# Channel mix on Trainium2: the order of work written by hand on four engines, and six PSUM banks for the quarter products

## The chip, the cores and the metric

The kernel runs on one core of a Trainium2 chip. A core has TensorE (matrix products, results in PSUM banks), VectorE and GpSimd (elementwise work), ScalarE (activations and copies), and queues from which SyncE starts DMA transfers. In the profile they are PE (with PEld for its weight loads), DVE, POOL, ACT and SP. The metric is the time of one execution on the device in microseconds (us); the time of a kernel is the median over several executions.

## The reference, cut to what matters

A batch of 8 sequences of 512 tokens with 512 channels goes through two layers, each a cross attention followed by a feed-forward part; each part adds its gated output to x. The change is in the last part, the channel mix (`_L1_ffn_ref`), and in the attention in front of it:

```python
x = x + tanh(g_xattn[1]) * _L1_xattn_ref(layernorm(x), ctx, ctx, mask, ...)
x = x + tanh(g_ffn[1]) * _L1_ffn_ref(layernorm(x), W_r, W_k, W_v, mu_r, mu_k)

# _L1_ffn_ref, for each sequence x of shape (512 tokens, 512 channels):
x_prev = x shifted by one token, with zeros in front
xr = mu_r * x + (1 - mu_r) * x_prev
xk = mu_k * x + (1 - mu_k) * x_prev
r = sigmoid(xr @ W_r.T)
k_act = square(relu(xk @ W_k.T))
out = r * (k_act @ W_v.T)
```

All of it is float32.

## The kernel before

**Stages.** x stays in SBUF for the whole kernel, as 32 tiles of 128 tokens. The program runs the first attention, a routed feed-forward part, the second attention, and the channel mix. Each attention is a loop over the 32 tiles. One pass of it is called a slot here, and it works on several tiles at once: the normalization of one tile, the scores of another, the transposed probabilities (`tps`, L328) and the output (`ops`, L363) of others. On VectorE a slot has the maxima of the scores (L303), the subtraction (L304), the sums (L309), the reciprocals (L316), the addition to x (L372), and the statistics of the layer normalization (`layernorm_stats`: L50 and L51, with small steps on GpSimd at L53 to L55, and two buffers for its temporary `bnst`); ScalarE makes the exponentials (L307) and copies (L333, L346), and GpSimd scales the probabilities (L317).

**The channel mix** handles one sequence ("batch" b, four tiles) at a time in three stages, each one product of two 512 x 512 matrices: the keys (k), the gates (g) and the values (v). k is xk times W_k, followed by Relu (L1010) and Square (L1011) on ScalarE, in the tile `kT`. g is xr times W_r, followed by Sigmoid (L1020) on ScalarE, in `r`. v is kT times W_v, followed on VectorE by the product with r (L1032) and by the gated addition to x (L1034, a scalar_tensor_tensor). Two finished quarters side by side are written to the output by one DMA of 512 KB (L1038).

What a batch needs ahead of that: the normalized tiles `xn` (ScalarE, L952), their transposes (TensorE into the bank `xnps`, L966; ScalarE copies them to `yT`, L967), and the mixes xk and xr in four chunks 0 to 3 each: a chunk is one scaled copy on ScalarE (L981) and one scalar_tensor_tensor on VectorE (L984). The four transposes of the tiles of a batch are called tr0 to tr3 here.

**Seven products.** Each stage multiplies with seven products of 256 x 256 quarters instead of eight. A quarter fits one PSUM bank (128 partitions x 512 elements). The left matrix gives A11, A12, A22 and four sums S1 to S4, the right one B11, B21, B22 and T1 to T4; these sums are made of quarters by additions and subtractions (`left`, L791 to L794; `right`, L802 to L805): by VectorE for kT (S), xr (`xrs`, S) and xk (`xks`, T), and once for the weights, by GpSimd for W_v and W_k and by VectorE for W_r. The products are called p1 to p7, and k.p3 is product p3 of the keys:

- p1 = A11 B11: ScalarE copies its bank (L839)
- p6 = S2 T2: VectorE adds it to p1 (L844), giving u2
- p7 = S3 T3: VectorE adds it to u2 (L849), giving u3
- p2 = A12 B21: VectorE adds it to p1 (L853): quarter 00 is finished
- p5 = S1 T1: ScalarE copies its bank (L860). GpSimd adds it to u2 (L861) and to u3 (L862): quarter 11 is finished
- p4 = A22 T4: VectorE subtracts it (L867): quarter 10 is finished
- p3 = S4 B22: VectorE adds it (L872): quarter 01 is finished

The order is p1, p6, p7, p2, p5, p4, p3. Each product is four matmuls of 128 x 256 at L824 (two halves of rows, two of the summed dimension); the profile shows each float32 matmul as two, so a product stands as x8. The intermediate results lie in temporaries `ctmp`. The banks of the products come from the pool `at_mm` with the tag mm, which has four and which the transposes use too. The pool `at_s`, two tiles of two banks each with the tag s, holds the attention's scores and is not used in the mix after the attention's end.

**The order of the work.** Within the attention and the mix, TensorE executes what it is given in the order of the program text (`tc.manual_schedule(engines={PE})`). The order of VectorE, ScalarE and GpSimd is chosen by the framework's scheduler, which can also move an instruction ahead of others that were written earlier. Once compiled, each engine executes its own queue in order, and an instruction that waits holds up all that stand behind it. The output DMAs and the loads are started from SP's queue.

The channel mix begins inside the last slots of the attention (`in_slot`): weights are loaded, the first eight tiles get their statistics, batch 0 is normalized, transposed and mixed, and the keys of batch 0 begin. After the last slot `run` does batch after batch: in the keys the statistics and the tiles of the next batch, of which three are transposed there and the fourth in the gates; after that the xk chunks and the sums of the next batch, then the xr chunks and sums, and the values.

Of the kernel before, what the change touches and what calls it, by code (L numbers as in the profile page):

```python
# [9 lines left out]
FP = mybir.dt.float32  # L10
# [7 lines left out]
P = 128  # L18
# [758 lines left out]
class SevenProducts:  # L777
# [9 lines left out]
    @staticmethod  # L787
    def left(w, sums, engine):

        s1, s2, s3, s4 = sums  # L790
        engine.tensor_tensor(s1, quarter(w, 0, 1), quarter(w, 1, 1), ALU.add)  # L791
        engine.tensor_tensor(s2, s1, quarter(w, 0, 0), ALU.subtract)
        engine.tensor_tensor(s3, quarter(w, 0, 0), quarter(w, 0, 1), ALU.subtract)
        engine.tensor_tensor(s4, quarter(w, 1, 0), s2, ALU.subtract)  # L794
        own = [quarter(w, 0, 0), quarter(w, 1, 0), quarter(w, 1, 1)]
        return dict(zip(SevenProducts.LEFT, own + [s1, s2, s3, s4]))

    @staticmethod
    def right(w, sums, engine):

        t1, t2, t3, t4 = sums
        engine.tensor_tensor(t3, quarter(w, 1, 1), quarter(w, 0, 1), ALU.subtract)  # L802
        engine.tensor_tensor(t1, quarter(w, 0, 1), quarter(w, 0, 0), ALU.subtract)
        engine.tensor_tensor(t2, quarter(w, 1, 1), t1, ALU.subtract)
        engine.tensor_tensor(t4, t2, quarter(w, 1, 0), ALU.subtract)  # L805
        own = [quarter(w, 0, 0), quarter(w, 1, 0), quarter(w, 1, 1)]
        return dict(zip(SevenProducts.RIGHT, own + [t1, t2, t3, t4]))

    def __init__(self, nc, at, a, b, finish):

        self.nc, self.at, self.a, self.b, self.finish = nc, at, a, b, finish
        self.pieces = iter(
            [self.p1, self.p6, self.p7, self.p2, self.p5, self.p4, self.p3]
        )
# [5 lines left out]
    def multiply(self, a, b):  # L820
        ps = self.at.p_mm.tile([P, 2, 256], FP, name="cps", tag="mm")
# [11 lines left out]
    def temporary(self, n):  # L833
        return self.at.pool.tile([P, 2, 256], FP, name="ctmp", tag=f"v{n}")

    def p1(self):
        ps = self.multiply("A11", "B11")
        self.q1 = self.temporary(0)
        self.nc.scalar.copy(self.q1, ps)  # L839

    def p6(self):
        ps = self.multiply("S2", "T2")
        self.u2 = self.temporary(1)
        self.nc.vector.tensor_tensor(self.u2, self.q1, ps, ALU.add)  # L844

    def p7(self):
        ps = self.multiply("S3", "T3")
        self.u3 = self.temporary(2)
        self.nc.vector.tensor_tensor(self.u3, self.u2, ps, ALU.add)  # L849

    def p2(self):
        ps = self.multiply("A12", "B21")
        self.nc.vector.tensor_tensor(self.q1, self.q1, ps, ALU.add)  # L853
        self.finish(0, 0, self.q1)

    def p5(self):
        nc = self.nc
        ps = self.multiply("S1", "T1")
        q5 = self.temporary(3)
        nc.scalar.copy(q5, ps)  # L860
        nc.gpsimd.tensor_tensor(self.u2, self.u2, q5, ALU.add)  # L861
        nc.gpsimd.tensor_tensor(q5, self.u3, q5, ALU.add)  # L862
        self.finish(1, 1, q5)

    def p4(self):
        ps = self.multiply("A22", "T4")
        self.nc.vector.tensor_tensor(self.u3, self.u3, ps, ALU.subtract)  # L867
        self.finish(1, 0, self.u3)

    def p3(self):  # L870
        ps = self.multiply("S4", "B22")
        self.nc.vector.tensor_tensor(self.u2, self.u2, ps, ALU.add)  # L872
        self.finish(0, 1, self.u2)


class ChannelMix:
# [5 lines left out]

    def __init__(self, cm, tc, es, ins, gate, out):
        self.cm, self.nc, self.tc, self.es = cm, cm.nc, tc, es
        self.ins, self.gate, self.out = ins, gate, out
        self.xn, self.yT, self.mix, self.sums = {}, {}, {}, {}

    def start(self):
# [12 lines left out]
        self.wk7 = SevenProducts.left(self.wk, [sums[:, i] for i in range(4)], nc.gpsimd)  # L901
# [5 lines left out]
    def sum_weights(self):  # L907
# [3 lines left out]
        self.wr7 = SevenProducts.right(self.wr, [sums[:, i] for i in range(4)], nc.vector)  # L911
# [3 lines left out]
        self.wv7 = SevenProducts.right(self.wv, sums, nc.gpsimd)  # L915
        self.kTs = [both[:, i] for i in range(3, 7)]

    def in_slot(self, s, attention, late):

        self.at = attention  # L920
        if not late:
            if NT - 1 <= s:
                self.k7.next(2)
            return
        if s == -1:
            self.start()
        if NT - 14 <= s < NT - 6:
            layernorm_stats(self.cm, self.at.norm, s - (NT - 14))
# [6 lines left out]
        if 0 <= i < TB:  # L935
            self.normalize(i)
        if s in (NT - 3, NT - 2):
            self.mixes(0, 1, slice(2 * (s - NT + 3), 2 * (s - NT + 3) + 2))
        if s == NT - 2:
            self.sum_mix(0, 1)  # L940
# [3 lines left out]
        if s == NT:  # L944
            self.sum_weights()
            self.mixes(0, 0)
            self.sum_mix(0, 0)

    def normalize(self, t):
        nc, cm = self.nc, self.cm  # L950
        self.xn[t] = xn = self.at.norm.tile([P, D], FP, name="xn")
# [17 lines left out]
    def mixes(self, b, m, chunks=slice(0, NC)):  # L969

        nc, yT = self.nc, self.yT[b]
        if chunks.start == 0:
# [7 lines left out]
        for c in range(NC)[chunks]:  # L980
            nc.scalar.activation(  # L981
# [197 lines left out]
```

## Time and profile before

| | |
|---|---|
| median of three runs | 1501.27 us (1497.16 to 1504.57) |
| the profiled execution | 1501.78 us, span in the trace 1499.6 us |
| mean granted TensorE clock | 0.99 |
| TensorE busy | 1420.2 us (95% of the span) |
| VectorE busy | 1034.0 us (69%) |
| ScalarE busy | 721.4 us (48%) |
| GpSimd busy | 547.8 us (37%) |
| in the mix alone (1200 to 1499.6 us): TensorE, VectorE, ScalarE, GpSimd busy | 281.6, 207.5, 133.4, 64.5 us |

Times in the trace count from the start of the span. The second attention ends near 1160 us; its last slots and the keys and gates of batch 0 lie between 1144 and 1200 us. From 1200 us on a batch takes some 40 us.

How the lines are to be read: a row of the page's slices has one digit for each fortieth of the span (37.5 us), the busy share in tenths. A line of the timeline gives the start, the duration, the engine, the line of the program, the operation, the names of what it writes and reads with their shapes, the count of merged instructions, and in brackets the idle time in front of it with what ended it. A line of the chain of waits gives start, duration, engine, and what the chain of work that ended last passes through.

### The profile page before, as it was taken

Reading aid. Unit: us, or ns where it says so; the run is one execution under the profiler, and the core shown is the slowest. Engines: PE = TensorE matmul, PEld = TensorE weight load, DVE = VectorE, ACT = ScalarE, POOL = GpSimd, SP = SyncE. Lnnn points to the kernel's source line nnn. Section 1 sums busy time; section 2 is a strip of 40 time slices with the busy share of each in tenths; the row PEclk is TensorE's granted clock in tenths of the full one; section 3 lists DMA queues with packets and bytes.
Section 4 is the critical chain, followed back from the end, with each engine's and each line's share of the span. In section 5 each row is a group of like instructions: output and inputs, shape, how many; then the busy total and the mean of one; then the engine's idle time right before and its main releaser. Section 6 shows DMA issues by size and latency. Waiting matters only on the chain.

```text
span 1499.6 us, 30719 instructions
## 1 busy us (share of the span) xinstructions
PE 1420.2 (95%) x13344; PEld 1003.2 (67%) x13344; DVE 1034.0 (69%) x1382; ACT 721.4 (48%) x983; POOL 547.8 (37%) x585
## 2 busy tenths in 40 slices
PE   7999999999988998999899999999997999999997
PEld 3456666666666787888545666666564788888886
DVE  3457777777777676766716777777778777777774
ACT  2246565565544445444224555555555455444432
POOL 2514333333333001555844554455335312222212
PEclk9999999999998999999999999999998999999999
DMA  9200000000000437433201000000000000000000
GB/s 303 86 9 22 22 22 23 22 23 23 22 22 23 131 121 235 119 100 96 100 0 56 2 1 1 1 2 1 1 30 1 1 28 29 29 28 28 29 29 29
DMA packets 44329, 69.33 MB, mean 46 GB/s; under 512 B 2859, under 2 KB 19755, under 8 KB 44195
## 3 DMA queue, kind: packets, MB, share of 16 engines
q1 hardware_dynamic: 43907, 67.37, 13.9%
q8 instruction: 105, 1.72, 0.5%
q14 instruction: 29, 0.24, 0.0%
q10 hardware_dynamic: 288, 0.00, 0.0%
HBM read 50.59 MB, written 16.78 MB: 45 GB/s over the span
## 4 chain that ended last, share of the span: by engine, by line
PE 75%; DVE 14%; ACT 5%; POOL 3%; issue 2%; DMA 1%; POOLq 0%; ACTq 0%; DVEq 0%
PE qps L255 15%; PE ops L363 13%; PE cps L824 9%; PE tps L328 7%; PE s L289 4%; PE aps L346 4%; PE vps L197 4%; PE rps L733 3%; PE kps L178 3%; PE ops L754 2%; PE l1ps L648 2%; PE xnps L246 2%; PE rlps L475 2%; DVE xk L984 2%; PE gps L621 2%
## 5 line engine op out<-in xcount | busy, mean ns | idle before, releaser
L317 POOL TENSOR_TENSOR pr<-pr,rs 128x1920 f32<-128x1920 f32 x64 | 217.6, 3400 | 451.6 <-ACT prT L333 348.2
L363 PE MATMUL ops<-wo,aT 128*128 128x512 f32 x512 | 243.1, 598 | 2.3 <-ACT aT L354 2.3
L255 PE MATMUL qps<-xnT,wq 128*128 128x512 f32 x512 | 236.3, 603 | 1.4 <-ACT xnT L247 1.4
L307 ACT ACTIVATE pr<-pr 128x960 f32<-128x960 f32 x128 | 128.3, 1003 | 207.5 <-DVE pr L304 207.3
L303 DVE TENSOR_REDUCE mx<-s 128x8 f32<-128x960 f32 x128 | 142.2, 1152 | 105.5 <-PE s L289 105.5
L309 DVE TENSOR_REDUCE sm<-pr 128x8 f32<-128x960 f32 x128 | 147.6, 1153 | 24.9 <-ACT pr L307 24.5
L255 PEld LDWEIGHTS qps<-xnT,wq 128*128 128x128 f32 x512 | 92.1, 189 | 101.1 <-issue 93.2
L328 PEld LDWEIGHTS tps<-ident,pr 128*120 128x120 f32 x1024 | 120.0, 142 | 58.6 <-issue 44.7
L363 PEld LDWEIGHTS ops<-wo,aT 128*128 128x128 f32 x512 | 92.4, 192 | 92.0 <-issue 88.1
L328 PE MATMUL tps<-ident,pr 128*120 128x128 f32 x1024 | 129.7, 281 | 21.0 <-DVE pr L304 17.9
L304 DVE TENSOR_TENSOR pr<-s,mx 128x960 f32<-128x960 f32 x128 | 141.6, 1148 | 0.0
L333 ACT COPY prT<-tps 120x1024 f32<-120x1024 f32 x128 | 124.1, 1015 | 36.4 <-PE tps L328 36.4
L746 POOL TENSOR_TENSOR r<-r,b 128x1024 f32<-128x1024 f32 x32 | 75.9, 2377 | 148.9 <-ACT r L745 148.9
L372 DVE SCALAR_TENSOR_TENSOR x<-ops,gates,x 128x512 f32<-128x512 f32 x64 | 48.1, 751 | 94.8 <-PE ops L363 94.8
L861 POOL TENSOR_TENSOR ctmp<-ctmp 128x512 f32<-128x512 f32 x24 | 33.6, 1401 | 202.8 <-DVE ctmp L849 96.8
L50 DVE BATCH_NORM_STATS2 bnst<-x 128x6 f32<-128x512 f32 x128 | 85.0, 685 | 17.2 <-DMA x<-in_x_dram 15.2
L247 ACT COPY xnT<-xnps 128x512 f32<-128x512 f32 x64 | 37.7, 589 | 81.7 <-PE xnps L246 81.7
L54 POOL TENSOR_TENSOR rstd<-ve,mhalf 128x1 f32<-128x1 f32 x128 | 72.0, 564 | 6.1
L346 PE MATMUL aps<-prT,v 120*32 120x128 f32 x2048 | 70.0, 276 | 2.4 <-ACT prT L333 2.4
L289 PE MATMUL s<-kT,qT 32*128 32x120 f32 x2048 | 71.1, 275 | 0.0
L289 PEld LDWEIGHTS s<-kT,qT 32*128 32x128 f32 x2048 | 65.6, 186 | 6.4 <-issue 6.3
L733 PE MATMUL rps<-ident,rT 128*128 128x128 f32 x512 | 61.9, 275 | 5.6 <-DVE rT L713 5.6
(141 smaller groups left out, 2490.2 us busy)
## 6 DMA issues: line engine op xcount, KB each, us to landing
w<-in_w_dram SPq DMA_DIRECT2D x32, 512.0 KB, 5.2
x<-in_x_dram SPq DMA_DIRECT2D x8, 1024.0 KB, 15.6
aside<-x SPq DMA_DIRECT2D x32, 256.0 KB, 2.0
x<-aside SPq DMA_DIRECT2D x8, 1024.0 KB, 10.5
out_dram<-x SPq DMA_DIRECT2D x16, 512.0 KB, 2.9
ctx<-in_ctx_dram SPq DMA_DIRECT2D x4, 960.0 KB, 11.7
wk<-in_wk_dram SPq DMA_DIRECT2D x3, 1024.0 KB, 9.3
wv<-in_wv_dram SPq DMA_DIRECT2D x3, 1024.0 KB, 5.4
```

The source lines that it names most:

```text
L255: nc.tensor.matmul(ps, self.wq[:, c, f * P : (f + 1) * P], self.xnT[b][:, c, :S], start=(c == 0), stop=(c == NC - 1),)
L289: nc.tensor.matmul(s[j // 2][:, j % 2, hc * LK : (hc + 1) * LK], self.qT[b][r : r + 32, hc, toks], self.kT[r : r + 32, hc, keys], start=no ...
L303: nc.vector.tensor_reduce(mx, sv, AX.X, ALU.max)
L304: nc.vector.tensor_tensor(pv, sv, mx.to_broadcast([P, 2, NC, LK]), ALU.subtract)
L307: nc.scalar.activation(pv, pv, AF.Exp, scale=SM_SCALE)
L309: nc.vector.tensor_reduce(sm[:, 2 * u : 2 * u + 2, :], pr[:, 2 * u : 2 * u + 2, :, :], AX.X, ALU.add,)
L317: nc.gpsimd.tensor_tensor(pr, pr, rs.to_broadcast([P, 4, NC, LK]), ALU.mult)
L328: nc.tensor.transpose(ps[:, jj, hc * P : (hc + 1) * P], pr[:, 2 * u + jj, hc, :], self.cm.ident,)
L333: nc.scalar.copy(prT[:, 2 * u : 2 * u + 2, :, :], ps.rearrange("p j (h t) -> p j h t", t=P),)
L346: nc.tensor.matmul(aps[32 * j : 32 * j + 32, hc, :], self.v[b // 2][:LK, b % 2, h * HD : (h + 1) * HD], prT[:, j, hc, :], start=True, stop ...
L363: nc.tensor.matmul(ops, self.aT[t][:, c, :], self.wo[:, c, :], start=(c == 0), stop=(c == NC - 1),)
L824: self.nc.tensor.matmul(ps[:, m, :], self.a[a][:, k, m * P : (m + 1) * P], self.b[b][:, k, :], start=(k == 0), stop=(k == 1),)
```

## The change

In the products:

- They write their results in place: the quarters of `kT`, of `r`, and, for the values, of two tiles `cv` take the part of the temporaries. p5's copy has a tile of its own (`q5`).
- The order is p1, p2, p6, p5, p7, p4, p3; in the values of the last batch p1, p6, p5, p7, p4, p3, p2. GpSimd's two additions follow p7 instead of p5.
- `bank()`: when the attention is over, every third product takes a bank of the tag s; the others take mm as before.

In the values: one scalar_tensor_tensor on VectorE makes c x gate x r (L1092), and a second instruction adds it to x (L1095): on GpSimd, and in the last batch's upper two quarters on VectorE. The last batch writes each finished quarter by its own DMA of 256 KB (L1100); the other batches write two quarters at a time as before (L1104).

In the order of the work: the statistics of all tiles move into the slots of the attention, tile s - 2 into slot s. `stage` hands out a list of other work among the seven products of a stage: in the keys of a batch its own xr chunks and their sums; in the gates the four transposes of the next batch, the sums of kT, and the next xk chunks; in the values the sums of these, and the normalizations of the batch after that. `mix.run()` is executed in the order of the text on TensorE, VectorE, ScalarE and GpSimd.

New line numbers: the products are at L848, the copies of p1 and p5 at L858 and L871, VectorE's additions at L862 (p2), L867 (p6), L875 (p7), L882 (p4) and L887 (p3), GpSimd's at L876 and L877; Relu and Square at L1068 and L1069, Sigmoid at L1079; normalization at L994, the copy to yT at L1009, the chunks at L1022 and L1025.

```diff
 class SevenProducts:
-    def left(w, sums, engine):            # four tensor_tensor at once
+    def left_steps(w, s1, s2, s3, s4, engine):   # a list of four steps
+        return [
+            step(s3, a11, a21, ALU.subtract),
+            step(s1, a21, a22, ALU.add),
+            step(s2, s1, a11, ALU.subtract),
+            step(s4, a12, s2, ALU.subtract),
+        ]
...
-    def __init__(self, nc, at, a, b, finish):
-        self.pieces = iter(
-            [self.p1, self.p6, self.p7, self.p2, self.p5, self.p4, self.p3]
-        )
+    def __init__(self, nc, psum, a, b, c, spare, finish=None, order="1265743"):
+        self.q1 = c[0, 1] if order.index("2") < order.index("6") else c[0, 0]
+        self.pieces = iter([getattr(self, "p" + n) for n in order])
...
     def multiply(self, a, b):
-        ps = self.at.p_mm.tile([P, 2, 256], FP, name="cps", tag="mm")
+        ps = self.psum()
...
+    def p5(self):
+        self.q5 = self.spare()
+        self.nc.scalar.copy(self.q5, self.multiply("S1", "T1"))
     def p7(self):
-        ps = self.multiply("S3", "T3")
-        self.u3 = self.temporary(2)
-        self.nc.vector.tensor_tensor(self.u3, self.u2, ps, ALU.add)
+        nc, u2, u3 = self.nc, self.c[0, 1], self.c[1, 0]
+        nc.vector.tensor_tensor(u3, u2, self.multiply("S3", "T3"), ALU.add)
+        nc.gpsimd.tensor_tensor(self.c[1, 1], u3, self.q5, ALU.add)
+        nc.gpsimd.tensor_tensor(u2, u2, self.q5, ALU.add)
     def p4(self):
-        ps = self.multiply("A22", "T4")
-        self.nc.vector.tensor_tensor(self.u3, self.u3, ps, ALU.subtract)
-        self.finish(1, 0, self.u3)
+        ps, c21 = self.multiply("A22", "T4"), self.c[1, 0]
+        self.finish(1, 1, self.c[1, 1])
+        self.nc.vector.tensor_tensor(c21, c21, ps, ALU.subtract)
+        self.finish(1, 0, c21)
...
 class ChannelMix:
     def in_slot(self, s, attention, stage):
-        if NT - 14 <= s < NT - 6:
-            layernorm_stats(self.cm, self.at.norm, s - (NT - 14))
+        if 0 <= s - 2:
+            layernorm_stats(self.cm, self.at.norm, s - 2)
...
         if s == NT:
+            self.k7.next()
+            layernorm_stats(self.cm, self.at.norm, NT - 1)
             self.sum_weights()
...
+            for t in range(TB, 2 * TB):
+                self.normalize(t)
...
+    def bank(self):
+        self.banks += 1
+        if self.alone and self.banks % 3 == 0:
+            ps = self.at.p_s.tile([P, 2, 512], FP, name="cps2", tag="s")[:, 0, :]
+            return ps.rearrange("p (m c) -> p m c", m=2)
+        return self.at.p_mm.tile([P, 2, 256], FP, name="cps", tag="mm")
...
     def values(self, b):
         def finish(i, j, c):
-            rv = quarter(r, i, j)
-            nc.vector.tensor_tensor(rv, c, rv, ALU.mult)
             xs = quarter(x, i, j)
-            nc.vector.scalar_tensor_tensor(xs, rv, self.gate, xs, ALU.mult, ALU.add)
+            nc.vector.scalar_tensor_tensor(
+                c, c, self.gate, quarter(r, i, j), ALU.mult, ALU.mult
+            )
+            (nc.vector if last and i == 0 else nc.gpsimd).tensor_tensor(xs, xs, c, ALU.add)
...
+        order = "1657432" if last else "1265743"
...
+    def stage(self, product, work):
+        for n in range(7):
+            product.next()
+            for _ in range(-(-len(work) // (7 - n))):
+                work.pop(0)()
...
     def run(self):
+        self.alone = True
         for b in range(B):
             if b > 0:
-                for t in ahead:
-                    layernorm_stats(self.cm, self.at.norm, t)
+                self.stage(self.keys(b), chunks(b, 0) + sums(b, 0))
...
+            squares = SevenProducts.left_steps(self.kT, *self.kTs, self.nc.vector)
+            work = list(squares)
+            if more:
+                tiles = [(TB * (b + 1) + i,) for i in range(TB)]
+                work = calls(self.transpose, *tiles) + work + chunks(b + 1, 1)
+            self.stage(self.gates(b), work)
+            work = []
+            if more:
+                work += sums(b + 1, 1)
+            if b + 2 < B:
+                work += calls(self.normalize, *[(TB * (b + 2) + i,) for i in range(TB)])
+            self.stage(self.values(b), work)
...
-    with ExitStack() as es, tc.manual_schedule(engines={mybir.EngineType.PE}):
+    with ExitStack() as es:
...
+        with tc.manual_schedule(engines={mybir.EngineType.PE}):
+            CrossAttention(...).run()
+        engines = mybir.EngineType
+        with tc.manual_schedule(
+            engines={engines.PE, engines.DVE, engines.Activation, engines.Pool}
+        ):
+            mix.run()
```

## The prediction

> **What bounds the kernel now.** I read the page first: the busy rows, the slices, the chain. Then the chain in order of time for the last stage, and the timeline of one batch there, engine by engine.
>
> ```profile
> PE 1420.2 (95%) x13344; PEld 1003.2 (67%) x13344; DVE 1034.0 (69%) x1382; ACT 721.4 (48%) x983; POOL 547.8 (37%) x585
> ...
> PE   7999999999988998999899999999997999999997
> ...
> PEclk9999999999998999999999999999998999999999
> ```
>
> TensorE is busy 95% of the span at full clock. The channel mix has the last 300 us (slices 33 to 40). The chain there:
>
> ```profile
> 1312.93 2.65 DVE xk L984 x4
> ...
> 1352.90 2.65 DVE xk L984 x4
> ```
>
> Every 40 us the chain leaves TensorE for VectorE, which makes the xk chunks there before it empties the bank that TensorE waits for. The timeline of TensorE, one batch earlier, has that wait in brackets:
>
> ```profile
> 1274.67 1.89 PE L824 MATMUL cps<-wrs,xr 128*128 128x256 f32 x8
> 1278.06 1.99 PE L824 MATMUL cps<-wr,xrs 128*128 128x256 f32 x8 [1.49 <-DVE ctmp L849]
> 1279.89 1.89 PE L824 MATMUL cps<-wv,kT 128*128 128x256 f32 x8
> 1281.61 3.62 PE L824 MATMUL cps<-wvs 128*128 128x256 f32 x16
> 1285.07 1.24 PE L824 MATMUL cps<-wv,kT 128*128 128x256 f32 x5
> ```
>
> Two products take 1285.07 - 1281.61 = 3.46, one 1.727 us; four transposes of a tile take 0.435. A batch of 21 products and 4 tiles needs 38.0 us of TensorE. It takes 39.98 (v.p1 at 1279.89 and next at 1319.87). The 2.0 between are one wait per batch: g.p3 needs the bank of g.p7, and VectorE empties it (L849) late. From v.p1 of batch 0 (1200.65) to that of batch 7 (1478.30) it is 277.65 us; TensorE alone would need 147 x 1.727 + 24 x 0.435 = 264.3. So **13.4 us are to be had there**.
>
> The second thing to see is how VectorE and GpSimd get in each other's way:
>
> ```profile
> 1289.85 1.58 POOL L861 TENSOR_TENSOR ctmp<-ctmp 128x512 f32<-128x512 f32 x1 [2.51 <-DVE ctmp L849]
> 1291.52 1.60 POOL L862 TENSOR_TENSOR ctmp<-ctmp 128x512 f32<-128x512 f32 x1
> ```
>
> ```profile
> 1290.23 0.68 DVE L853 TENSOR_TENSOR ctmp<-ctmp,cps 128x512 f32<-128x512 f32 x1
> 1290.94 1.04 DVE L1032 TENSOR_TENSOR r<-ctmp,r 128x512 f32<-128x512 f32 x1
> 1292.02 1.64 DVE L1034 SCALAR_TENSOR_TENSOR x<-r,gates,x 128x512 f32<-128x512 f32 x1
> 1293.59 0.68 DVE L1032 TENSOR_TENSOR r<-ctmp,r 128x512 f32<-128x512 f32 x1
> ```
>
> L853 has one input in PSUM and runs its 0.68 beside L861. L1032 and L1034 have both inputs in SBUF: each ends 0.55 after the GpSimd instruction in front of it (1291.43 + 0.55 = 1291.98; 1293.12 + 0.54 = 1293.66). L862 in turn is stretched from 1.26 to 1.60 by L1032. Such instructions exclude each other whole, and take turns.
>
> **The change part by part.** A queue walk: each engine's compiled order, each instruction at the later of its queue and its producers. Durations from the tile views: VectorE 0.68 (next one 0.60 later), scalar_tensor_tensor 0.745 (0.67), GpSimd 1.26 (1.35), ScalarE 0.57 to 0.62 for copies, Relu, Square, Sigmoid, 0.71 for a mix chunk; a product is read 0.2 after its end. For before, this walk gives 39.94 per batch against 39.98 measured, with the wait at g.p3: the method holds to 0.1 us.
>
> *Steady batch.* TensorE's work is unchanged, 38.0. Six banks instead of four: g.p3 no longer waits for g.p7. VectorE loses little: a finished quarter of the values cost 0.68 + 0.745, and now costs one scalar_tensor_tensor of 0.745; the add of x (4 per batch) goes to GpSimd, 1.26 each, which has 10 such adds instead of 6. What is late next, in us from the start of g.p1:
> - The third transpose, tr2, needs the bank of k.p3, emptied at 5.7: 1.46 late. tr3 needs the bank of g.p1, whose copy stands on ScalarE behind the last Relu and Square of the keys (each waits for its quarter): 1.27 late. So g.p7 ends at 13.3, not 10.6.
> - g.p7 is added by VectorE until 14.2; GpSimd's two adds follow, the first until 16.0 (held by xk chunk 0), and hold xk chunk 1 until 16.6. ScalarE has Sigmoids in front of mix chunks 2 and 3: each waits for VectorE's g.p4 (17.2) and g.p3 (19.9), so the last xk chunk ends at 21.9, 5 us after the gates' products.
> - VectorE then works without a break: T3, T1, v.p2 and its gate step, T2, v.p6, T4, v.p7 until 27.6. Then quarter 11 from GpSimd (29.0), gate step, v.p4, gate step, v.p3, gate step until 33.2, two of them held by the adds of x. The next xr chunks 0 and 1 are held by the last two adds of x: 34.9 and 36.6, where they would be done by 34.5.
> - k.p2 (37.2), Relu, Square and mix chunks 2 and 3 on ScalarE, k.p7 until 42.4, GpSimd until 44.1, k.p4, S2 (held until 46.0), k.p3 until 46.66. That frees tr2 of the next batch: 46.72 - 5.78 = **40.94 us per batch**.
>
> At this spot a rule of the Trainium skill can be weighed. GPSIMD Engine Reference, Key points: VectorE is structurally about 2x faster in elementwise work, and the two contend where VectorE has two SBUF inputs; no price is given for that. It speaks against the moved add. By the 2x alone, the adds would lie beside VectorE's work on an engine that is 37% busy, and the walk without their exclusion gives 38.0: 13.4 us won. By the rows above each add stops a VectorE instruction, and the walk gives 40.94. I take the rows. The page Perfetto Trace Analysis, Identifying Performance Opportunities, takes consistent bubbles as a sign of too little PSUM: by it, too, two more banks would give 38.0. The row says that L849 is late because of VectorE's queue; two banks more move the wait to tr2.
>
> Six periods of 40.94 and the last (no transposes, no chunks ahead) of 38.2 are 283.8, against 277.65: **+6.2 us**.
>
> *Handover, 1144 to 1200.*
>
> ```profile
> 1151.21 1.59 POOL L803 TENSOR_TENSOR wv<-wv 128x512 f32<-128x512 f32 x1
> ```
>
> ```profile
> 1155.03 3.64 PE L328 MATMUL tps<-ident,pr 128*120 128x128 f32 x16 [6.92 <-DVE pr L304]
> ```
>
> The compiled order puts one more VectorE subtraction (the sum T3 of batch 0) ahead of the maximum (L303, at 1151.61 now) that tps follows. GpSimd's L803 holds it until 1153.4: the maximum and tps start 1.7 later, the idle is 8.6. Given back afterwards: 1.0 and 0.7 of TensorE's waits at 1184.9 and 1197.1, and small ones, since the tiles of batch 1 are normalized earlier and the banks are six. v.p1 of batch 0 comes at 1200.1 instead of 1200.65: **-0.5**, between -2 and +2.
>
> *Tail.* The last order ends with p2, and writes quarters. From v.p1: products end at 12.1, VectorE, which has 11 steps after v.p7 and is held by four GpSimd instructions, at 17.2; before 1495.69 - 1478.30 = 17.4. From there to the end of the span it was 3.9 with 512 KB; the page has 2.9 for 512 KB and 2.0 for 256 KB (aside<-x): 3.0 to 3.9, I take 3.5. **-0.6**.
>
> *Attention.* The statistics for the mix now share two buffers with the attention's own from slot 2 on; the order shows 16 of the attention's no longer hoisted ahead of it, and 19 slots with two statistics where before only three slots held two. Such a slot before:
>
> ```profile
> 839.71 1.29 DVE L50 BATCH_NORM_STATS2 bnst<-x 128x6 f32<-128x512 f32 x2
> 840.91 0.30 DVE L51 BATCH_NORM_AGGREGATE mv<-bnst 128x2 f32<-128x6 f32 x2
> 841.57 2.22 DVE L303 TENSOR_REDUCE mx<-s 128x8 f32<-128x960 f32 x2 [0.36 <-PE s L289]
> ```
>
> VectorE still waits 0.36 for TensorE, and the slot is 11.46 as without: **0**. Were that cover gone, 16 slots x at most 0.8 = 13 us. Quarters written in place, Relu and Square in place: the same instructions, 0. The four normalizations in a row (2.9) lie in ScalarE's idle from 24.4 to 30.8. SP's two last transfers become four; before them nothing on its queue is moved past anything, and nobody waits for the others.
>
> Sum: 0 - 0.5 + 6.2 - 0.6 = +5.1. The profiled execution took 1501.78 (span 1499.6 and 2.2 around it), so 1506.9; it stands 0.5 over the median of 1501.27: **1506.5**. A measurement here can tell about 0.5% from no change, 7.5 us: below 1493.8 is faster, above 1508.8 slower.
>
> **The rivals.**
> 1. *TensorE sets the pace* (faster). About 5 us per batch of the loop are holds between VectorE and GpSimd. If 2.9 of them don't come, the loop falls under 38.0 and the banks do their work: 264.3 instead of 277.65, with the rest -14.5, so 1487. For it: VectorE's work is 27 us of 38, GpSimd's 13. Against: L1034 at 1.64, and xr chunks (L984) of up to 3.88 in the tile view.
> 2. *GpSimd gets the better of the turns* (slower). If its next add starts without the gap of 0.09, the walk gives 41.5; if a held VectorE instruction needs 0.1 more to restart, 41.6; both some 42. From 41.3 on it is over the 0.5%. 7 x 0.6 to 1.1 more: 1511 to 1515. Against: the turns alternate in the rows above.
> 3. *The loop closes as before* (no change): ScalarE or GpSimd a little quicker than walked, 40.0 per batch; only handover and tail count: 1500.
>
> **How the numbers follow.** Forecast 0.46 (1502 to 1511; 0.32 of it below 1508.8), GpSimd's turns 0.22, the loop as before 0.16, TensorE's pace 0.16 (with part of the holds left, 1487 to 1496; 0.13 of it below 1493.8). Faster 0.13; same 0.03 + 0.16 + 0.32 = 0.51; slower 0.14 + 0.22 = 0.36. The range leaves out most of rival 1 and the upper end of rival 2: 1493 to 1515.
>
> **What would show it.** Right: TensorE waits of 1 to 1.5 us before the third and fourth transposes of each gates stage, released by k.p3's add (L887) and g.p1's copy (L858); v.p1 to v.p1 40.9; xr chunks 0 and 1 at 1.7 us beside L1095; idle of 8 to 9 us before tps at 1156. Wrong: v.p1 to v.p1 under 39.5, no waits before transposes, L1095 beside unstretched chunks; or slots of the attention above 11.46.

## The result and the profile after

The changed kernel takes 1506.03 us (median of 8 runs, 1504.21 to 1510.9) against 1499.07 us of the kernel before (8 runs, 1497.16 to 1504.57): the ratio is 1.0046, with a 95% interval of 1.0032 to 1.0060. It is slower by 0.46%, clear of the noise by this interval; that lies inside the 0.5% that the prediction called no change, close to its edge. The forecast was 1506.5.

The page after, the same three rows as before:

```profile
PE 1417.3 (94%) x13344; PEld 1001.0 (67%) x13344; DVE 1045.6 (70%) x1352; ACT 724.6 (48%) x983; POOL 591.4 (39%) x615
...
PE   7999999999988998999899999999997999999997
...
PEclk9999999999999999999999999999998999999999
```

VectorE has 30 instructions fewer than before and is busy 11.6 us longer; GpSimd has 30 more and is busy 43.6 us longer. TensorE does the same work. The timeline of TensorE in one gates stage of the changed kernel (start, duration, instruction; in brackets the idle time in front of it and what ended it):

```profile
1310.88 0.66 PE L1008 MATMUL xnps<-ident,xn 128*128 128x128 f32 x4 [1.32 <-DVE kT L887]
1312.68 0.66 PE L1008 MATMUL xnps<-ident,xn 128*128 128x128 f32 x4 [1.14 <-ACT r L858]
1313.17 5.44 PE L848 MATMUL cps<-wrs,xrs 128*128 128x256 f32 x24
1318.45 1.89 PE L848 MATMUL cps<-wrs,xr 128*128 128x256 f32 x8
```

The old wait before g.p3 is gone (`cps<-wr,xrs` follows without brackets). In its place the third and fourth transposes wait for their banks, the one for k.p3's add (L887), the other for g.p1's copy (L858): 2.46 us per batch where 1.49 stood. v.p1 follows v.p1 after 40.98 us (1280.90, 1321.91, 1362.89, ...).

Where the loop is tight is read from the chain of waits between two such transposes (start, duration, what the chain passes through; "issue" is time in which an engine waits for nothing that the profile shows):

```profile
1337.60 0.69 DVE cv L887
1338.28 0.02 issue
1338.31 1.26 DVE cv L1092
1339.57 2.34 DVE xr L1025 x2
1341.91 0.61 DVE kT L862
1342.52 0.02 issue
1342.54 0.64 ACT kT L1068
...
1343.74 0.71 ACT xr L1022
...
1345.15 0.68 DVE kT L867
...
1347.01 0.69 DVE kT L875
...
1347.83 1.60 POOL kT L876
```

In the order of the text VectorE finishes the values of a batch (L1092), makes two xr chunks of the next one (L1025), and only then empties k.p2's bank (L862). ScalarE makes Relu and Square of that quarter (L1068, L1069) before it can turn to xr chunk 2 (L1022), and VectorE, which is given that chunk ahead of k.p6's add (L867), waits for it. The additions that GpSimd makes meanwhile show why L1092 and L1025 are long. Timeline of GpSimd, and below it VectorE's gate step of quarter 11, a little earlier:

```profile
1333.96 1.27 POOL L877 TENSOR_TENSOR cv<-cv,q 128x512 f32<-128x512 f32 x1
...
1337.76 1.27 POOL L1095 TENSOR_TENSOR x<-x,cv 128x512 f32<-128x512 f32 x1 [0.63 <-DVE cv L1092]
1339.65 1.71 POOL L1095 TENSOR_TENSOR x<-x,cv 128x512 f32<-128x512 f32 x1 [0.63 <-DVE cv L1092]
```

```profile
1334.03 1.74 DVE L1092 SCALAR_TENSOR_TENSOR cv<-cv,gates,r 128x512 f32<-128x512 f32 x1 [1.44 <-POOL cv L876]
```

The add at 1337.76 ends at 1339.03; VectorE's L1092 that began at 1338.31 ends 0.54 later. The add at 1339.65 overlaps the two xr chunks, which take 2.34 instead of the 1.4 of two chunks that nothing holds. The gate step of quarter 11 is held by L877, GpSimd's second addition of p5: it takes 1.74 instead of 0.75 and ends 0.54 after it.

### The profile page after: what moved, and what is told of

Same layout as the page of the kernel before. It is cut to its first block, busy times and chain, and to the rows that moved or that the text cites. A ratio compares the mean times of both kernels' runs of the same rounds, so it can differ in the third digit from the quotient of the medians.

```text
span 1504.1 us, 30766 instructions
## 1 busy us (share of the span) xinstructions
PE 1417.3 (94%) x13344; PEld 1001.0 (67%) x13344; DVE 1045.6 (70%) x1352; ACT 724.6 (48%) x983; POOL 591.4 (39%) x615
## 4 chain that ended last, share of the span: by engine, by line
PE 77%; DVE 11%; ACT 5%; issue 4%; POOL 3%; DMA 1%; POOLq 0%; ACTq 0%
PE qps L255 15%; PE ops L363 13%; PE cps L848 10%; PE tps L328 7%; PE aps L346 4%; PE s L289 4%; PE vps L197 4%; PE kps L178 4%; PE rps L733 3%; PE ops L754 2%; PE l1ps L648 2%; PE xnps L246 2%; PE rlps L475 2%; PE gps L621 2%; PE l2ps L700 1%
## 5 line engine op out<-in xcount | busy, mean ns | idle before, releaser
L303 DVE TENSOR_REDUCE mx<-s 128x8 f32<-128x960 f32 x128 | 142.2, 1152 | 96.1 <-PE s L289 96.1
L1095 POOL TENSOR_TENSOR x<-x,cv 128x512 f32<-128x512 f32 x30 | 43.9, 1465 | 62.7 <-DVE cv L1092 62.7
## 6 DMA issues: line engine op xcount, KB each, us to landing
x<-aside SPq DMA_DIRECT2D x8, 1024.0 KB, 10.6
```

Source lines behind the costliest of these rows:

```text
L303: nc.vector.tensor_reduce(mx, sv, AX.X, ALU.max)
```

## The experiments

All were timed against the kernel before on the same chip, whose median in these groups lay between 1498.9 and 1501.7; "ratio" is that to the kernel before, with its 95% interval (medians of different groups compare less well), and "period" is the distance of v.p1 from v.p1 in the middle batches of the profile. "From first to last" is v.p1 of batch 0 to v.p1 of batch 7.

| kernel | median us | ratio | period us | first to last us |
|---|---|---|---|---|
| before | 1499.07 | 1 | 39.98 | 277.65 |
| changed | 1506.03 | 1.0046 (1.0032 to 1.0060) | 40.98 | 284.19 |
| e1, adds of x on VectorE | 1512.08 | 1.0076 (1.0059 to 1.0093) | 41.35 | 290.12 |
| e2, four banks | 1508.32 | 1.0048 (1.0033 to 1.0064) | 41.48 | 287.17 |
| e7, before with six banks | 1494.81 | 0.9964 (0.9952 to 0.9975) | 39.98 | 272.80 |
| e8, no adds of x | 1488.75 | 0.9924 (0.9906 to 0.9942) | 38.46 | 267.03 |
| e3, transposes apart | 1498.24 | 0.9992 (0.9984 to 1.0000) | 39.70 | 276.50 |
| e4, p5's adds on VectorE | 1495.45 | 0.9976 (0.9968 to 0.9985) | 39.69 | 275.11 |
| e5, transposes and chunks | 1490.60 | 0.9939 (0.9925 to 0.9952) | 38.54 | 268.48 |
| e6, e5 with e4 | 1484.43 | 0.9895 (0.9879 to 0.9910) | 38.02 | 264.36 |
| e9, other last order | 1506.87 | 1.0053 (1.0037 to 1.0070) | 40.98 | 285.87 |
| e11, scheduler's order | 1486.18 | 0.9916 (0.9900 to 0.9933) | 38.01 | 264.33 |
| e13, e6 with four banks | 1488.39 | 0.9920 (0.9905 to 0.9935) | 38.65 | 268.19 |
| e15, e6 with e1 | 1486.14 | 0.9900 (0.9878 to 0.9922) | 38.02 | 264.36 |

**Is it the moved add?** e1 gives the adds of x back to VectorE, and e8 leaves them out.

```diff
-            (nc.vector if last and i == 0 else nc.gpsimd).tensor_tensor(xs, xs, c, ALU.add)
+            nc.vector.tensor_tensor(xs, xs, c, ALU.add)
```

> The changed kernel with the additions to x (L1095) on VectorE in every batch; GpSimd keeps only its six additions per batch. Queue walk: VectorE has no break between the gates and the end of the values, so 4 x 0.6 us more on its queue delay the xr chunks, k.p3's add and the bank of the third transpose: 41.6 us per batch (wait before the third transpose 2.1, before the fourth 1.3), tail 0.8 longer; some 5.5 us slower than the changed kernel, 1511.5. Rival (the moved add is what costs, because GpSimd and VectorE exclude each other): with the adds back on VectorE the loop falls to between 38.0 and 39.98 us per batch, 1487 to 1499.

It became slower, not faster: 1512.08 us. The wait before the third transpose grew from 1.3 to 1.66; the fourth kept its 1.14. So the rival falls that moving the adds is what costs: undoing the move makes the loop longer, by 0.37 us per batch. Only 2.4 us of the 5.9 by which its way from first to last is longer are the loop; the other 3.5 are two stretches of slow TensorE in its profile (last section). GpSimd's other six additions still hold VectorE in e1 (quarter 11's gate step takes 1.74 there too); e4 below takes these away. The row of stretches tells why the move gives VectorE so little (busy us and count of TensorE, its weight loads, VectorE, ScalarE, GpSimd, then clock, DMA share and GB/s; first the changed kernel, then e1):

```profile
1281.00:1322.00 41.00, 38.54 (x186) 33.50 (x185) 30.40 (x40) 20.12 (x34) 14.61 (x12) 1.00 0.07 26
```

```profile
1281.00:1322.00 41.00, 38.20 (x184) 33.20 (x183) 30.26 (x43) 20.11 (x34) 8.33 (x8) 1.00 0.07 26
```

In 41 us VectorE is busy 30.4 with the adds moved away and 30.3 with them: what it saves it loses again, held by the very adds that it gave away. (With the adds on VectorE the last two gate steps take 0.75 each and the pair of xr chunks 1.41, against 1.27, 1.26 and, in the same view, 2.41.) That the 0.4 us per batch that the move is still worth come from where the held time falls is not shown.

```diff
-            (nc.vector if last and i == 0 else nc.gpsimd).tensor_tensor(xs, xs, c, ALU.add)
+            if last:
+                nc.vector.tensor_tensor(xs, xs, c, ALU.add)
```

> The changed kernel without the addition to x in batches 0 to 6 (x goes out as it was; this part of the computation is left out; the last batch adds on VectorE). Queue walk: VectorE's instructions in front of k.p3's add are no longer held by GpSimd's adds, the waits before the transposes vanish, TensorE sets the pace at 38.0 us per batch: 264.3 us from the first to the last batch instead of 284.2, about 19 us faster than the changed kernel, 1487. Rival (the order of the queues alone sets the loop, the adds fill gaps): 40 to 41 us per batch, 1500 to 1506.

Without the adds no wait before the transposes is marked in the profile, and the time is 1488.75 us; the period is 38.46 rather than 38.0, since a short stop between the third and the fourth transpose remains:

```profile
1302.05 1.39 PE L1008 MATMUL xnps<-ident,xn 128*128 128x128 f32 x8
```

Undisturbed, the two transposes of that line take 1.04. In this order the four adds per batch cost 2.5 us of the loop on GpSimd (40.98 against 38.46) and 2.9 on VectorE (e1): VectorE has no room for them between the values and the next keys. That is a statement on the order as much as on the adds; e11 below shows an order that has room.

**Is it the banks?** e2 takes them from the changed kernel (`if False:` in `bank`), e7 gives them to the kernel before, with no other edit.

> The changed kernel with four banks (tag mm alone) for the products and transposes. Queue walk: 41.4 us per batch, with waits before k.p3 (1.35, by k.p6's add) and g.p2 (1.3, by k.p3's add) in place of those before the third and fourth transposes: 2.6 us slower than the changed kernel, 1508.6. Rival 1 (the two banks do pay for themselves and the old wait comes back on top of the new ones): 1.5 to 2.0 us more per batch, 1517 to 1520. Rival 2 (the banks are worth nothing at all here): 1506.

```diff
     def multiply(self, a, b):
-        ps = self.at.p_mm.tile([P, 2, 256], FP, name="cps", tag="mm")
+        ps = self.bank()
+    def bank(self):
+        SevenProducts.banks += 1
+        if SevenProducts.alone and SevenProducts.banks % 3 == 0:
+            ps = self.at.p_s.tile([P, 2, 512], FP, name="cps2", tag="s")[:, 0, :]
+            return ps.rearrange("p (m c) -> p m c", m=2)
+        return self.at.p_mm.tile([P, 2, 256], FP, name="cps", tag="mm")
...
     def run(self):
+        SevenProducts.alone = True
```

> The kernel before with nothing changed but the banks: every third product takes a bank of the tag s once the attention is over. Queue walk: the wait before g.p3 goes, and the same loop of VectorE, ScalarE and GpSimd makes TensorE wait elsewhere, before the next batch's transposes and products of the keys: 39.94 us per batch as now, so 1499 like the kernel before. Rival (a lack of banks is the cause of the wait): TensorE's 38.0 us per batch, 13 us faster than the kernel before, 1486.

e2's loop came out as walked: period 41.48, with waits of 1.0 before k.p3 and before g.p2 and 0.5 before a transpose (the first ended by the copy of k.p5, L871, and not by k.p6's add). By the profile's period two banks are worth 0.5 us per batch to the changed kernel; the medians differ by 2.3 us that way, but the ratios (1.0048 and 1.0046) do not tell the two kernels apart.

e7 was expected to change nothing, and it was faster by 0.36%. The timeline of TensorE of e7 shows which half of the expectation held (middle batches):

```profile
1337.45 0.66 PE L975 MATMUL xnps<-ident,xn 128*128 128x128 f32 x4 [1.15 <-DVE ctmp L853]
1337.95 1.89 PE L824 MATMUL cps<-xks,wk 128*128 128x256 f32 x8
1340.21 0.66 PE L975 MATMUL xnps<-ident,xn 128*128 128x128 f32 x4 [0.37 <-ACT xn L961]
```

In the middle batches the wait has moved from g.p3 to the transposes in the keys, and the period is 39.98, exactly that of the kernel before. But the first two periods are 38.02 and 38.57 instead of 39.24 and 40.00, 2.65 us less, and the wait of 0.74 before the first v.p1 (at 1197.09 in the kernel before) is gone, which is 1.0 us more. That fits a TensorE that runs ahead once, until all six banks are full: some 3.6 us, won once and not per batch. The walk looked at the steady batch alone.

The profiled executions are 7.1 us apart, and not all of that is the banks. The first v.p1 comes at 1198.42 instead of 1200.65, but 1.2 of these 2.2 us are TensorE's clock. The same four matmuls behind the idle before tps, first in the kernel before and then in e7:

```profile
1158.46 3.15 PE L363 MATMUL ops<-wo,aT 128*128 128x512 f32 x4
```

```profile
1158.46 1.92 PE L363 MATMUL ops<-wo,aT 128*128 128x512 f32 x4
```

From 1158.4 to 1161.6 the granted clock was 0.59 in the one and 0.98 in the other. Another 1.8 are a slow stretch of TensorE in the kernel before (last section), and 0.4 an order of VectorE that only one of its batches has. The ratio, over 16 executions of e7, is worth 5.4 us (3.7 to 7.2).

**Is it the order?** e3 moves only the transposes of the gates, e5 also the xk chunks, and e11 leaves everything to the scheduler except TensorE's order.

```diff
-            self.stage(self.gates(b), work)
+            # the product behind which each of transposes, squares and chunks stands
+            at = [0, 1, 2, 3] + [2, 2, 3, 3] + [4, 4, 5, 6]    # e3
+            at = [0, 1, 2, 3] + [2, 2, 3, 3] + [3, 4, 4, 5]    # e5
+            self.stage(self.gates(b), work, at if more else [0, 1, 2, 3])
```

`stage` takes this list as a new argument. In this writing the changed kernel has [0, 0, 1, 1], [2, 2, 3, 3] and [4, 4, 5, 6].

> The changed kernel with one edit in the gates: the four transposes of the next batch stand behind p1, p2, p6 and p5 (one each) instead of two behind p1 and two behind p2. Queue walk: g.p1's copy is no longer what the fourth transpose waits for; one wait is left, 1.5 us before g.p6 by k.p3's add; 39.6 us per batch, 8 us faster than the changed kernel, 1498. Rival (the waits are only where a loop of VectorE and GpSimd shows, so they move and nothing is won): 40.9 us per batch, 1506.

> The changed kernel with the transposes behind p1, p2, p6 and p5 of the gates, and the four xk chunks behind p5, p7, p7 and p4 instead of p7, p7, p4 and p3. Queue walk: 38.3 us per batch (one wait of 0.2 left), 17 us faster than the changed kernel, 1489. Rival (earlier chunks only collide earlier with GpSimd's additions): 39.6 us per batch as with the transposes alone, 1498.

Both met their walk. In e3 one wait of TensorE was left, in front of g.p6:

```profile
1307.21 1.99 PE L848 MATMUL cps<-wrs,xrs 128*128 128x256 f32 x8 [1.29 <-DVE kT L887]
```

The period is 39.70 and the time 1498.24 us: three transposes put one or two products later take back what the change had cost. With three of the four xk chunks one product earlier as well (e5) it is 38.54 and 1490.60 us. So the waits were not the mark of a loop that nothing in the gates can shorten.

```diff
         with tc.manual_schedule(
-            engines={engines.PE, engines.DVE, engines.Activation, engines.Pool}
+            engines={engines.PE}
         ):
             mix.run()
```

> The changed kernel with the order of the text kept for TensorE alone in the mix; VectorE, ScalarE and GpSimd get the order that the framework's scheduler chooses for the same work. Queue walk over the compiled order: the scheduler puts the bank's adds, the xk chunks and the next batch's xr chunks earlier, and no wait of TensorE is left in the loop: 38.0 us per batch, 264 from the first to the last, 20 us faster than the changed kernel, 1486. Rival (the hand order is as good as the scheduler's, and the moved adds of x cost what they cost in any order): 40 to 41 us per batch, 1500 to 1506.

This undoes the hand-written order of VectorE, ScalarE and GpSimd, and nothing else: same adds on GpSimd, same banks, same products. The time is 1486.18 us, 1.3% under the changed kernel, and the loop runs at TensorE's 38.01. So the hand-written order is what made the change slower; all the rest of it together, in the scheduler's order, is 0.84% faster than the kernel before. Which part of that rest (the banks, the moved adds, the order of the products, the writing in place, the earlier statistics) wins this was not taken apart. VectorE's timeline there shows what the scheduler does otherwise (v.p1 is at 1312.89):

```profile
1315.45 0.74 DVE L1025 SCALAR_TENSOR_TENSOR xr<-yT,mu,xr 128x512 f32<-128x512 f32 x1
1316.12 0.67 DVE L887 TENSOR_TENSOR r<-r,cps 128x512 f32<-128x512 f32 x1
1316.71 2.06 DVE L1025 SCALAR_TENSOR_TENSOR xr<-yT,mu,xr 128x512 f32<-128x512 f32 x3
...
1330.17 1.27 DVE L1092 SCALAR_TENSOR_TENSOR cv<-cv,gates,r 128x512 f32<-128x512 f32 x1
1331.36 0.68 DVE L862 TENSOR_TENSOR kT<-kT,cps 128x512 f32<-128x512 f32 x1
1332.14 0.69 DVE L867 TENSOR_TENSOR kT<-kT,cps 128x512 f32<-128x512 f32 x1
```

The four xr chunks of the next batch lie at the start of the values. They are behind it when the last gate step (L1092, held as before: 1.27) is done, so k.p2's add (L862) follows at once, and k.p6's add (L867) 0.8 later instead of 3.3. In the hand-written order the chunks stand in the keys, behind the adds of x. Which of the scheduler's moves is worth how much was not tested one by one.

**Fewer additions on GpSimd.** e4 lets VectorE read p5's bank itself, so that GpSimd has only the adds of x and ScalarE no copy of p5; e6 is e5 with e4; e13 is e6 with four banks; e15 is e6 with the adds of x on VectorE too.

```diff
     def p5(self):
-        self.q5 = self.spare()
-        self.nc.scalar.copy(self.q5, self.multiply("S1", "T1"))
+        self.q5 = self.multiply("S1", "T1")
     def p7(self):
-        nc.gpsimd.tensor_tensor(self.c[1, 1], u3, self.q5, ALU.add)
-        nc.gpsimd.tensor_tensor(u2, u2, self.q5, ALU.add)
+        nc.vector.tensor_tensor(self.c[1, 1], u3, self.q5, ALU.add)
+        nc.vector.tensor_tensor(u2, u2, self.q5, ALU.add)
```

> The changed kernel with p5's two additions on VectorE, which reads p5's bank itself: no copy by ScalarE, no addition by GpSimd except the four of x per batch. VectorE gets 6 more instructions per batch, each with one input in PSUM. Queue walk: 40.0 us per batch (waits 0.7 before the first transpose by k.p5's addition and 1.1 before the fourth by g.p1's copy), tail 0.7 shorter: 7 us faster than the changed kernel, 1499. Rival (VectorE, 70% busy, becomes the bound, as it did with the adds of x): 41 to 42 us per batch, 1506 to 1513.

> The transposes and xk chunks placed as in the run before, and p5's additions on VectorE from the bank. Queue walk: no wait of TensorE left in the loop, 38.0 us per batch (264.3 from the first to the last), tail 0.7 shorter: 20 us faster than the changed kernel, 1486, and 13 to 14 faster than the kernel before. Rival (VectorE, now with 24 instructions of products per batch, holds the loop): 40 us per batch, 1499.

> The run with transposes and chunks placed apart and p5's additions on VectorE, with four banks (tag mm alone) instead of six. Queue walk: waits of 0.9 come back before g.p1 (by k.p5's addition) and before g.p3 (by g.p5's addition), 40.0 us per batch, 13 us slower than with six banks, 1498. Rival (the banks are worth no more here than in the changed kernel, where they gave 0.5 us per batch): 38.0 to 38.5, 1484 to 1488.

> The run with transposes and chunks placed apart and p5's additions on VectorE, and the adds of x on VectorE too, so that GpSimd adds nothing in the mix. VectorE had 134.1 us of busy time in 160 in that run; without GpSimd's holds it loses some, with four adds of 0.6 per batch it gains some. Queue walk: still no wait of TensorE, 38.0 us per batch, the end 0.3 later: 1484 to 1485, no difference that the median can tell from 1484.4. Rival (the adds of x on VectorE cost here what they cost in the changed kernel, 0.4 us per batch and more): 38.4 to 39 us per batch, 1488 to 1492.

e4 gained 10.6 us on the changed kernel instead of 7 (period 39.69; the wait before the first transpose, which the walk had, is not there). Six more instructions per batch on VectorE did not make it the bound: each reads PSUM and takes 0.67 to 0.69, and the gate step of quarter 11, which GpSimd's L877 had held, takes 0.75 instead of 1.74. e6 met its walk: no wait of TensorE in the loop, 1484.43 us, **1.05% faster than the kernel before (0.90 to 1.21%) and, by the medians, 1.4% faster than the changed one**. It has the lowest median of these kernels; the intervals of e11 and e15 overlap with its own. e13 missed its walk: four banks cost 0.63 us per batch there (a wait of 0.4 by g.p1's copy is all that is marked), not 2.0. Its rival (38.0 to 38.5 us, 1484 to 1488) was nearer, missed by 0.15 us per batch. In e15 VectorE's busy time over the same 160 us is that of e6 (first e6, then e15):

```profile
1240.00:1400.00 160.00, 160.00 (x774) 140.91 (x774) 134.11 (x192) 79.86 (x130) 25.86 (x21) 1.00 0.07 27
```

```profile
1240.00:1400.00 160.00, 160.00 (x774) 140.92 (x773) 133.63 (x207) 80.86 (x132) 0.42 (x4) 1.00 0.07 27
```

Fifteen instructions more, and 0.5 us less: GpSimd's adds of x took from VectorE what they spared it. In this loop, which waits for TensorE alone (38.02 both), the place of the adds made no difference that the time shows.

**The end.** e9 gives the last batch the order of the others.

> The changed kernel with the last batch's values in the order of the others (p1, p2, p6, p5, p7, p4, p3); its quarters still go out one by one. Queue walk: VectorE's last step ends 16.8 us after the last v.p1 instead of 17.2, then the same DMA of 256 KB: the stretch from the last v.p1 to the end of the span is 0.4 shorter than the changed kernel's 20.97, 20.6; the median cannot tell it, 1505.6. Rival (the other order does shorten the end, because p2's quarter needs nothing of GpSimd and finishes soon after its product): the stretch becomes 1 to 2 us longer, 22 to 23.

From the last v.p1 to the end of the span it takes 20.54 us against 20.97 in the changed kernel and 21.30 before. The rest of the change at the end (quarters written one by one, the new gate step) wins 0.8, and the other order of products gives 0.4 of it back, in one profiled execution each; the median (1506.87) cannot show that.

## Why the prediction was right, point by point

- **The steady batch.** 40.94 us were walked and 40.98 measured; the two waits were walked as 1.46 and 1.27 and measured as 1.32 and 1.14, at the two transposes named and by the two instructions named. First to last was to be 283.8 and was 284.19. Up to v.p7 the steps that the walk names come within 0.2 us of it. Behind that two of its terms are wrong by a microsecond each, and cancel. The last gate step ends 34.5 us after the start of g.p1, where 33.2 was walked: all three gate steps from quarter 11 on are held, not two, the first by L877. And the two xr chunks behind it were walked as 1.7 us each, both held; the pair took 2.34, so they end at 36.8, where 36.6 was walked. That the period came within 0.04 is in this part luck.
- **The base that this was set against was mis-sized.** 277.65 contained one batch of 42.22 us instead of 39.98. There TensorE ran slowly for some 7 us (last section), which is 1.8 of the difference; the rest is that in this one batch VectorE makes the xk chunks ahead of L844, so that TensorE waits 2.05 us at g.p4. Without the slow stretch it is 275.8, and the loop costs 8.4 us where 6.2 were forecast. The median of the kernel before was also taken too high, 1501.27 of three executions; over eight it is 1499.07. So the change was to cost 5.2 us and cost 7.0, from a base that was 2.2 lower. That the two errors took each other off, and 1506.5 met 1506.03, was luck too.
- **The handover.** tps was to start 1.7 later. It starts at 1155.80 against 1155.03; the changed kernel was 0.9 ahead already at the scores of the last tile (1143.10 against 1143.99), and as much at 840 us (L303 at 840.68, below, against 841.57), so that lead is older. That makes 1.7, and the idle is 9.14 where 8.6 were walked. The waits at 1184.9 and 1197.1 went as said: v.p1 of batch 0 at 1198.94, 0.8 earlier by the same reckoning, for 0.5 forecast.
- **The end.** -0.6 was forecast and -0.3 measured. The gate step of quarter 11 took 1.74 us, held by GpSimd's second addition (L877), and two more were held at 1.26, three where the prediction had four; VectorE ended 17.6 after v.p1 instead of 17.2, and the end of the span came 3.4 later instead of 3.5.
- **The attention.** A slot with two statistics still has the 0.36 of waiting for TensorE that covers them:

```profile
838.82 1.29 DVE L50 BATCH_NORM_STATS2 bnst<-x 128x6 f32<-128x512 f32 x2
840.02 0.30 DVE L51 BATCH_NORM_AGGREGATE mv<-bnst 128x2 f32<-128x6 f32 x2
840.68 2.22 DVE L303 TENSOR_REDUCE mx<-s 128x8 f32<-128x960 f32 x2 [0.36 <-PE s L289]
```

- **The rule on GpSimd.** The GPSIMD Engine Reference of the Trainium skill (Key points) puts VectorE at about twice GpSimd's speed (here 0.68 us against 1.26) and lets the two contend where VectorE has two SBUF inputs. By its factor alone the moved adds were free; by the rows they were not. e1 and e15 give the price that this section lacks: an add of 1.26 us on GpSimd took from VectorE about the 0.6 that it had saved it. e1 also corrects the prediction, which told the held instructions as the reason for the loss: with the adds on VectorE the same order was slower still.
- **The rule on banks.** Perfetto Trace Analysis of the Trainium skill (Identifying Performance Opportunities) says that consistent bubbles can mean too little PSUM. In the loop of the kernel before, e7 spoke against it: the period did not move by 0.01. In the changed kernel the wait does stand before tr2, as the prediction had it, and the prediction missed nothing by leaving out e7's head start: there the first period is 40.99 already. But the banks are worth something where the order no longer holds the loop: some 4 us between e13 and e6.
- **The rivals.** TensorE's pace (1487) needed 2.9 us of holds to stay away. It was the right target by the wrong way: e11 reaches 38.01 with the gate steps held as before (1.27 and 1.73 us), in an order that does the next batch's xr chunks earlier.

## What to carry to other kernels

A hand-written order on the engines that serve the bottleneck has to be walked with the waits of each queue, not only listed by what depends on what: the same work, adds and banks ran at 40.98 us per batch in the written order and at 38.01 in the scheduler's. Place each piece by the bank or buffer whose release it delays, and work that is not needed soon (the next batch's chunks) ahead of the crowded stretch, not in it. An addition handed from VectorE to GpSimd was no relief here, because VectorE's instructions beside it had two SBUF inputs and were held; p5's additions were cheaper on VectorE straight from the bank (e4) than as a copy on ScalarE and two additions on GpSimd, although VectorE is the busier engine.

## What the runs showed that was not expected

TensorE slows down for a few microseconds now and then, in the middle of an otherwise even loop. In the kernel before (the first row is the stretch, with the clock as the third number from the end; then the timeline of TensorE):

```profile
1436.00:1443.00 7.00, 6.20 (x21) 5.19 (x22) 5.26 (x8) 2.57 (x5) 2.86 (x2) 0.76 0.01 2
```

```profile
1436.80 3.15 PE L824 MATMUL cps<-wrs,xr 128*128 128x256 f32 x8 [2.05 <-DVE ctmp L844]
1439.74 2.46 PE L824 MATMUL cps<-wr,xrs 128*128 128x256 f32 x8
```

The two products take 3.15 and 2.46 us instead of 1.89 at a granted clock of 0.76 in the mean, with 1.00 before and behind. e1 has two such places, of which this is the second:

```profile
1479.72 7.11 PE L848 MATMUL cps<-wrs,xrs 128*128 128x256 f32 x24 [2.14 <-ACT kT L1068]
```

Three products take 7.11 us instead of 5.44; the other (7.13 at 1356.68) is in another batch, and e9 has one too (7.13 at 1233.64). Each is worth 1.7 to 1.8 us. In finer windows each of the places in these two traces is the same event: the granted clock is 0.50 for some 3.4 us, and 1.00 around it (in the kernel before 0.78 from 1436.8 to 1438, 0.50 up to 1440, 0.56 up to 1441, then 1.00; the first place of e1 has 0.97, three times 0.50, 0.82 and 1.00 in the microseconds from 1356). Half speed for 3.4 us loses 1.7. All four begin behind waits of TensorE of 1.1 to 2.1 us, and e6, e8, e11, e13 and e15, which have no wait above 0.5 us from 1200 us on, show none; but most such waits are followed by no slow stretch, and what starts one stays open. One profiled execution can hold one more or one less of them than another, which is as much as some of the terms above.

A second surprise was the head start: extra buffers that leave the steady period of a loop exactly as it was still shortened the whole once, by some 3.6 us in the profile.
